# Two graph layers by Strassen products on one core: the next image's transposed h is turned and summed in another phase

## The chip, the cores and the metric

The kernel runs on one core of a Trainium2 chip. The metric is the device time in microseconds of one execution; three executions of the kernel before gave 2360.97, 2363.22 and 2365.91 us, and their median, 2363.22, is the time before. The profile is of one more execution, whose span was 2354.3 us.

## The reference

There are 32 independent images (the batch). Each has a 512 x 512 matrix `x` (nodes by features) and a 512 x 512 adjacency `adj`. Two layers follow each other; everything is in 32-bit floats.

```python
# x, adj: [32, 512, 512]; nodemask: [32, 512]; W: [512, 1024]; Wqk: [512, 1024]; Wv: [512, 512]
# layer 0
h   = maximum(layernorm(x), 0)                      # eps 1e-5, over features
deg = sum(adj, -1, keepdims=True)
agg = einsum('bij,bjf->bif', adj, h) / maximum(deg, 1e-6)
x1  = x + relu(einsum('bnf,of->bno', concatenate([h, agg], 2), W))
# layer 1
h1  = maximum(layernorm(x1), 0)
q, k = split(h1 @ Wqk, 2, -1)
v    = h1 @ Wv
agg  = einsum('bij,bjd->bid', adj, k * nodemask[:, :, None])
w    = nodemask / sqrt(512) * einsum('bid,bid->bi', q, agg)
out  = x1 + softmax(w, axis=1)[:, :, None] * v
```

## The kernel before

Each 512 x 512 product is one level of Strassen's scheme: seven products of 256 x 256 blocks instead of eight. The factors stand in "slots": four for the blocks and three more for sums of blocks. `left_sums` and `right_sums` make those sums with four adds or subtractions each.

```python
def left_sums(s, on=None):
    return [
        lambda: add(s(4), s(2), s(3), on), lambda: sub(s(6), s(0), s(2), on),
        lambda: sub(s(5), s(4), s(0), on), lambda: sub(s(2), s(1), s(5), on),
    ]

def product(name, terms, place, finish):
    def m(k, p, first):                 # product k: 4 matmuls for each term
        ...
        yield                           # a step ends here
    pp = mm_tile(f"pp_{name}")          # a PSUM tile [128, 2, 256]; the pool has 8
    yield from m(1, pp, True)
    c11 = place(0, 0)
    copy(c11, pp)                       # ScalarE
    pr = mm_tile(f"pr_{name}")
    yield from m(2, pr, True)
    finish(0, 0, c11, pr, c11)          # VectorE
    yield from m(6, pp, False)          # goes on in pp
    ...                                 # k = 5, 7, 3 in the same manner, with a third tile pq
    yield from m(4, pp, False)
    finish(1, 0, None, pp, None)        # VectorE's last read of pp

def run(phase, n, plan):
    for i in range(n):
        if phase is not None:
            next(phase)                 # the matmuls of step i
        for f in plan.get(i, []):       # what the plan hangs on step i, for all engines
            f()
```

For image i the main loop runs four phases. A phase is a stream of TensorE work in steps, and a `Plan` hangs other engines' instructions on the steps. Engines take their instructions in the order in which they are recorded.

- **O** (`layer0_out`, tiles `pp_o`, `pr_o`, `pq_o`; 14 steps): h·W1 and adj·Y, giving x1 in `xu`. Reads hT as the left factor.
- **V** (`layer1_tv`, tiles `ptv`; 14 steps): the "joint product" of image i-1, two levels of Strassen, h1 by Wqk's and Wv's product matrix, giving `tv`.
- **U** (`layer1_u`, 7 steps): adj·(masked h1) of image i, into the buffer that held x1.
- **Y** (`layer0_y`, 7 steps): h·W2 of image i+1. Reads hT and its sums.

`hT` is the transposed h of the next image, in one buffer (half of the constant tile `wide`). The rows of h are normalised, written to scratch in HBM, read back in another order (`to.read`), and then turned in 32 x 32 blocks on VectorE (`turn`, two halves); then four `sums` fill the slots of Strassen's sums. The adjacency (`aT`) and h1 (`h1T`) go the same way.

```python
class FrontH:                           # h of one image
    def turn(self, h):
        self.to.turn(h, hT)             # VectorE, L280 of the kernel
    def sums(self, i):
        left_sums(of(hT))[i]()          # VectorE, L94 and L97

class FrontH1:                          # x1 and h1 of one image
    def keep(self):                     # x1 to scratch, 1 MB: dx<-xu
        nc.sync.dma_start(out=self.x1, in_=X[self.b].rearrange("p c f -> p (c f)"))
    def write(self, c):                 # normalise a quarter (ScalarE), send it: dh1T<-h1m
        normalize(self.rows(c), ...)
        nc.sync.dma_start(out=self.to.d[c]..., in_=self.rows(c))
    def mask(self, c):                  # ScalarE, in place: waits for the store of the quarter
        nc.scalar.activation(self.rows(c), self.rows(c), AF.Copy, scale=mraw[:, c, self.b:self.b + 1])

def layer0_out(b, w1):
    def finish(r, c, o, p, s):
        dst = X[b][:, 2 * r:2 * r + 2, ts(c, H)]
        if s is not None:
            add(o, p, s)
            p = o
        nc.vector.scalar_tensor_tensor(dst, p, 0.0, dst, op0=ALU.max, op1=ALU.add)   # L442

def layer1_tv(b):                       # 7 products of 7 matmul pairs, in 4 PSUM tiles each
    ...
    yield from parts(1, pp, True, keep(0))     # keep: ScalarE copies out
    yield from parts(2, pr, True, plus(0))     # plus: VectorE adds from PSUM
    yield from parts(6, pp, False, keep(1))
    yield from parts(5, pq, True, keep5)
    yield from parts(7, pp, False, keep(3))
    for n in range(4):
        add(part(3, n), part(3, n), m5[n])
    yield from parts(3, pq, False, plus(1))
    yield from parts(4, pp, False, keep(2))
```

`Post` is what follows V for image i-1: `recombine` makes the blocks of `tv` from the products (seven adds for the query half of `tv`, and seven for its value half), `dot`, `scores` and the softmax, then `apply` scales the value rows, `add_x1` adds x1 by an accumulating DMA of GpSimd, and `store` writes the output.

Of the kernel before, what the change touches and what calls it, by code (L numbers as in the profile page):

```python
# [22 lines left out]
def kernel(  # L23
# [72 lines left out]
    def sub(o, a, b, on=None):  # L96
        (on or nc.vector).tensor_tensor(o, a, b, op=ALU.subtract)  # L97
# [11 lines left out]
    def right_sums(s, on=None):  # L109
        return [  # L110
            lambda: sub(s(4), s(1), s(0), on), lambda: sub(s(6), s(3), s(1), on),
            lambda: sub(s(5), s(3), s(4), on), lambda: sub(s(1), s(2), s(5), on),
        ]

    def of(t):
        return lambda i: t[:, i]
# [133 lines left out]
    def shift(t, a=0, b=C):  # L250
        mv, rstd, nmr = t
        nc.vector.scalar_tensor_tensor(  # L252
            nmr[:, a:b], mv[:, a:b, 0], -1.0, rstd[:, a:b], op0=ALU.mult, op1=ALU.mult
        )
# [391 lines left out]
    stream = Stream()  # L646
# [5 lines left out]
    def chain(p, f, n):  # L652


        p.at(n(0), f.stats, 2)
        p.at(n(0), shift, f.t, 0, 2)
        p.at(n(0), f.write, 0)
        p.at(n(1), f.stats, 3)
        p.at(n(1), variance, f.t, 2, 4)
        p.at(n(1), f.write, 1)  # L660
        p.at(n(2), shift, f.t, 2, 4)
        p.at(n(3), f.write, 2)
        p.at(n(3), f.mask, 0)
        p.at(n(4), f.write, 3)
        p.at(n(4), f.keep)
        p.at(n(4), f.mask, 1)
        p.at(n(5), f.masked_sums, 0)
        p.at(n(5), f.mask, 2)
        p.at(n(6), f.mask, 3)
# [179 lines left out]
    with tc.manual_schedule(engines=engines):  # L849
        weights, mvR = start()  # L850
        post = None
        for i in range(B):
            more, last = i + 1 < B, i + 1 == B
            if i > 0:

                p = Plan()
                right_y = right_sums(of(Y[i]), nc.gpsimd)
                p.at(0, right_y[0])
                p.at(0, right_y[2])
                for k in (1, 3):  # L860
                    p.at(1 + k // 2, FA[i].sums, k, nc.gpsimd)
                    p.at(1 + k // 2, right_y[k])
                if i == 1:
                    for k, g in enumerate(weights[4:]):
                        p.at(3 + 2 * k, g)
                    fa = FA[2]
                    for h in range(2):
                        for c in range(2):
                            p.at(2 * h + c, fa.sum, 2 * h + c)
                            p.at(4 + 2 * h + c, fa.write, 2 * h + c)  # L870
                        p.at(2 + 2 * h, fa.degrees, h)
                    FH[3] = FrontH(3)
                    p.at(9, FH[3].load, 0)
                    p.at(10, FH[3].load, 1)
                f1 = F1[i - 1]
                if post is not None:
                    for k in (5, 6):
                        p.at(0, post.recombine, k, None, 1)
                p.at(0, f1.turn, 0)
                p.at(1, f1.turn, 1)  # L880
                if post is not None:
                    for c in range(C):
                        p.at(2 + c, post.apply, c)
                    p.at(3, post.add_x1, 0)
                    p.at(5, post.add_x1, 1)
                    p.at(9, post.store, 0)
                    p.at(11, post.store, 1)
                for k in range(4):
                    p.at(2 + k, f1.sums, k)
                for k in range(4):  # L890
                    p.at(5 + k, f1.inner_sums, k, 0, 7)
                for n in range(4):
                    p.at(2 * n + 1, stream.load)
                if 1 < i and i + 2 < B:
                    fh = FH[i + 2]
                    for c in range(C):
                        p.at(7 + c, fh.stats, c)
                        p.at([11, 12, 13, 13][c], fh.write, c)
                    p.at(10, variance, fh.t)
                    p[11].insert(0, lambda t=fh.t: shift(t))  # L900
                if more:
                    th = FH[i + 1]
                    p.at(5, th.to.read, 0)
                    p.at(6, th.to.read, 1)
                    p.at(11, th.turn, 0)
                f = F1[i] = FrontH1(i)
                p.at(12, f.stats, 0)
                p.at(12, f.stats, 1)
                p.at(13, variance, f.t, 0, 2)
                run(layer0_out(i, stream.take), 14, p)  # L910


                post = Post(i - 1, F1[i - 1])
                p = Plan()
                p.at(0, f.stats, 2)
                p.at(0, shift, f.t, 0, 2)
                p.at(0, f.stats, 3)
                p.at(1, variance, f.t, 2, 4)
                if last:
                    p.at(1, FA[i].factor)  # L920
                p.at(3, shift, f.t, 2, 4)
                for c in range(C):
                    p.at([2, 3, 5, 6][c], f.write, c)
                    p.at([7, 7, 8, 9][c], f.mask, c)
                p.at(6, f.keep)
                for k in range(4):
                    p.at([9, 10, 10, 11][k], f.masked_sums, k)
                if i + 2 < B:
                    fa = FA[i + 2] = FrontA(i + 2)
                    p.at(2 if i > 1 else 11, fa.load, 0)  # L930
                    p.at(3 if i > 1 else 13, fa.load, 1)
                if i == 1:
                    fh = FH[3]
                    for c in range(C):
                        p.at(4 + c, fh.stats, c)
                        p.at(9 + c, fh.write, c)
                    p.at(7, variance, fh.t)
                    p[9].insert(0, lambda t=fh.t: shift(t))
                if more:
                    p.at(3, th.turn, 1)  # L940
                exchanged = FA[i + 1] if more else f
                p.at(6, exchanged.to.read, 0)
                p.at(7, exchanged.to.read, 1)
                for k in range(7):
                    p.at(12 + k // 4, post.recombine, k, 0, 0)
                run(layer1_tv(i - 1), 14, p)


            p = Plan()
            if i == 0:  # L950
                fh = FH[2]
                for c in range(C):
                    p.at(c, fh.stats, c)
                p.at(3, variance, fh.t)
                p.at(4, shift, fh.t)
                p.at(4, weights[0])
                p.at(5, fh.write, 0)
                p.at(6, fh.write, 1)
                p.at(5, weights[1])
                p.at(2, FA[1].to.read, 0)  # L960
                p.at(3, FA[1].to.read, 1)
            elif more:
                for k in range(7):
                    p.at(k // 4, post.recombine, k, 1, 0)
                for c in range(C):
                    p.at(2 + c // 2, post.dot, c)
                p.at(4, post.scores)
                p.at(4, post.maximum)
                for k in range(4):
                    p.at(5 + k // 2, th.sums, k)  # L970
                p.at(6, post.shift)
                if i + 2 < B:
                    late = 2 if i == 1 else 0
                    for c in range(C):
                        p.at(1 + c + late, fa.sum, c)
                    p.at(3 + late, fa.degrees, 0)
                    if i > 1:
                        p.at(5, fa.degrees, 1)
            else:
                p.at(0, f.turn, 0)  # L980
                for k in range(3):
                    p.at(1, f.inner_sums, k, 0, 2)
                p.at(1, f.turn, 1)
                for k in range(4):
                    p.at(2 + k // 2, f.sums, k)
                p.at(4, f.inner_sums, 3, 0, 2)
                for k in range(4):
                    p.at(5 + k // 2, f.inner_sums, k, 2, 7)
# [5 lines left out]
            if more:  # L994
                p = Plan()
# [5 lines left out]
                if i > 0:  # L1001
                    p.at(1, post.exponents)
                    p.at(2, post.row_sum)
                    p.at(4, post.weights)
                    for k in range(5):
                        p.at(3 + (k + 1) // 2, post.recombine, k, None, 1)
                p.at(2, FA[i].factor)
                if i == 0:
                    p.at(0, fh.write, 2)
# [22 lines left out]
        p = Plan()  # L1032
# [71 lines left out]
```

## Time and profile before

| | before |
|---|---|
| median of three | 2363.22 us |
| profiled span | 2354.3 us |
| TensorE clock granted, mean | 0.996 |
| TensorE, VectorE, ScalarE, GpSimd busy | 2263.0, 1946.8, 1078.4, 495.3 us |
| DMA moved | 463.65 MB, 197 GB/s over the span |
| `dx<-xu` (x1 to scratch), issue to landing | 6.3 us, 32 times |
| `dh1T<-h1m` (h1 to scratch), issue to landing | 3.2 us, 128 times |

In the profile an instruction is named by its engine, the line of the kernel, its operation and its tiles, `out<-in`, with buffer numbers left out. Where a helper records the instruction, the line is the helper's: L94 and L97 are all adds and subtractions, L100 all copies of ScalarE, L130 all matmuls but V's, L467 V's. `wide` holds hT, `shT` the rows of h that are to be turned into it, `xu` x and x1, `m_tv` the copies of V's product 5. A wait is put down to the instruction that released it last. TensorE's own time line is the one to read for the end of the program; a gap on another engine costs something only if TensorE waits for it later.

### The profile page before, as it was taken

The page shows a single profiled execution, that of the slowest core. Times are in us where ns is not written, and L with a number is a line of the kernel's source. Part 1 is how long each engine was busy: PE and PEld are TensorE (multiplying, and loading weights), DVE is VectorE, ACT ScalarE, POOL GpSimd, SP SyncE. Part 2 cuts the span into 40 slices and gives each one's busy share as a digit, 9 for nine tenths or more (in the row PEclk, how much of TensorE's full clock was granted, in tenths as well). Part 3 has the DMA queues.
Part 4 walks back from the last instruction along what each step waited for, and adds up shares of the span by engine and source line. Part 5 has one row for each costly group of instructions (what it writes and reads, how often), then busy time and mean ns, then how long its engine had stood idle before and what let it go on. Part 6 is the DMA issues. An engine that isn't in the chain of part 4 may idle for free.

```text
span 2354.3 us, 32391 instructions
## 1 busy us (share of the span) xinstructions
PE 2263.0 (96%) x10372; PEld 1966.8 (84%) x10372; DVE 1946.8 (83%) x3619; ACT 1078.4 (46%) x2031; POOL 495.3 (21%) x453
## 2 busy tenths in 40 slices
PE   7999999999999999999999999999999999999995
PEld 6788888888888888888888888888888888888884
DVE  6698788888898887898888988888888889888878
ACT  4454443544444544444444445444454444455332
POOL 0102222112222122222022221222220222211222
PEclk9999999999999999999999999999999999999998
DMA  9877877777978778777779787788777797877662
GB/s 219 229 198 182 229 199 197 202 199 187 240 185 200 205 184 216 215 191 202 194 184 242 184 202 202 182 217 213 195 200 199 182 240 189 202 198 199 144 161 67
DMA packets 409593, 463.65 MB, mean 197 GB/s; under 512 B 37680, under 2 KB 271152, under 8 KB 405328
## 3 DMA queue, kind: packets, MB, share of 16 engines
q1 hardware_dynamic: 400176, 428.56, 69.2%
q0 software_dynamic: 8928, 32.51, 7.4%
q8 instruction: 82, 1.34, 0.2%
q14 instruction: 87, 0.71, 0.1%
q10 hardware_dynamic: 320, 0.52, 0.1%
HBM read 293.93 MB, written 167.51 MB: 196 GB/s over the span
## 4 chain that ended last, share of the span: by engine, by line
DVE 37%; DMA 23%; PE 21%; ACT 10%; issue 3%; SPq 3%; POOL 2%; DVEq 0%; ACTq 0%; POOLq 0%
DVE tv L94 12%; DMA dh1T<-h1m 6%; PE pp_o L130 5%; PE pp_y L130 5%; DVE st L242 4%; ACT tv L100 4%; DMA tv<-dx 3%; DMA shT<-dhT 3%; DVE tv L541 3%; DMA sh1T<-dh1T 3%; PE ptv L467 3%; ACT h1m L258 3%; PE pq_y L130 3%; DMA daT<-a 3%; DVE h1T L97 3%
## 5 line engine op out<-in xcount | busy, mean ns | idle before, releaser
L467 PE MATMUL ptv<-mv,h1T 128*128 128x256 f32 x3136 | 690.5, 380 | 17.1 <-DVE xu L442 14.2
L467 PEld LDWEIGHTS ptv<-mv,h1T 128*128 128x128 f32 x3136 | 593.9, 190 | 108.5 <-DVE xu L442 26.0
L94 DVE TENSOR_TENSOR tv<-tv 128x256 f32<-128x256 f32 (+1 forms) x644 | 315.7, 518 | 10.6
L130 PE MATMUL pp_y<-wide 128*128 128x256 f32 x1024 | 245.8, 383 | 32.6 <-DVE wide L97 32.6
L100 ACT ACTIVATE tv<-ptv 128x512 f32<-128x512 f32 x496 | 241.3, 537 | 62.2 <-PE ptv L467 61.2
L97 DVE TENSOR_TENSOR h1T<-h1T 128x512 f32<-128x512 f32 (+2 forms) x195 | 259.6, 1344 | 1.2
L130 PEld LDWEIGHTS pp_y<-wide 128*128 128x128 f32 x1024 | 193.5, 191 | 68.0 <-issue 43.0
L130 PE MATMUL pp_o<-y,aT 128*128 128x256 f32 x1024 | 242.5, 380 | 1.0 <-POOL y L97 0.9
L130 PE MATMUL pp_u<-h1m,aT 128*128 128x256 f32 x1024 | 242.1, 379 | 1.4 <-ACT xu L100 1.4
L130 PE MATMUL pp_o<-w,wide 128*128 128x256 f32 x992 | 234.5, 379 | 2.3 <-DMA w<-dw 2.3
L130 PEld LDWEIGHTS pp_u<-h1m,aT 128*128 128x128 f32 x1024 | 194.7, 190 | 28.4 <-ACT xu L100 1.8
L130 PEld LDWEIGHTS pp_o<-y,aT 128*128 128x128 f32 x1024 | 194.2, 190 | 28.8 <-POOL y L97 2.9
L130 PEld LDWEIGHTS pp_o<-w,wide 128*128 128x128 f32 x992 | 188.7, 190 | 28.0 <-issue 2.7
L97 POOL TENSOR_TENSOR y<-y 128x512 f32<-128x512 f32 x124 | 194.8, 1571 | 18.4 <-DVE y L94 16.0
L550 POOL PARTITION_ALL_REDUCE gtop<-top x32 | 22.2, 692 | 824.7 <-DVE top L547 824.7
L100 ACT ACTIVATE o<-pp_o 128x512 f32<-128x512 f32 x96 | 57.3, 597 | 301.5 <-PE pp_o L130 301.5
L94 DVE TENSOR_TENSOR tv<-tv,m_tv 128x512 f32<-128x512 f32 x124 | 69.2, 620 | 141.9 <-ACT tv L100 138.9
L248 POOL TENSOR_TENSOR rstd<-rstd,mhalf 128x2 f32<-128x2 f32 (+1 forms) x96 | 78.4, 817 | 503.4 <-DVE rstd L247 503.4
L258 ACT ACTIVATE n<-n,nmr,rstd 128x512 f32<-128x512 f32 x120 | 88.3, 805 | 189.5 <-DVE nmr L252 134.5
L97 DVE TENSOR_TENSOR h1m<-h1m 128x512 f32<-128x512 f32 x128 | 85.3, 688 | 105.5 <-ACT h1m L379 105.5
L100 ACT ACTIVATE xu<-pp_u 128x512 f32<-128x512 f32 x128 | 76.4, 597 | 199.6 <-PE pp_u L130 195.9
L94 DVE TENSOR_TENSOR tv<-ptv,tv 128x512 f32<-128x512 f32 x248 | 142.2, 614 | 2.9 <-PE ptv L467 2.9
(113 smaller groups left out, 3458.7 us busy)
## 6 DMA issues: line engine op xcount, KB each, us to landing
w<-dw SPq DMA_DIRECT2D x217, 256.0 KB, 4.7
xu<-in_x_dram SPq DMA_DIRECT2D x128, 256.0 KB, 4.8
a<-in_adj_dram SPq DMA_DIRECT2D x256, 128.0 KB, 3.3
dh1T<-h1m SPq DMA_DIRECT2D x128, 256.0 KB, 3.2
dx<-xu SPq DMA_DIRECT2D x32, 1024.0 KB, 6.3
sh1T<-dh1T SPq DMA_DIRECT2D x256, 128.0 KB, 5.0
shT<-dhT SPq DMA_DIRECT2D x248, 128.0 KB, 4.2
daT<-a SPq DMA_DIRECT2D x124, 256.0 KB, 4.8
```

Of the source, the lines that this page charges most:

```text
L94: (on or nc.vector).tensor_tensor(o, a, b, op=ALU.add)
L97: (on or nc.vector).tensor_tensor(o, a, b, op=ALU.subtract)
L100: nc.scalar.activation(o, i, AF.Copy)
L130: nc.tensor.matmul(p[:, rc, :], lt[:, LEFT[k], dk, ts(rc, P)], right[:, dk, :], start=first and n == 0, stop=True, skip_group_check=True,)
L242: nc.vector.bn_stats(st, src)
L248: nc.gpsimd.tensor_tensor(rstd[:, a:b], rstd[:, a:b], mhalf[:, a:b], op=ALU.pow)
L258: nc.scalar.activation(o, i, AF.Relu, scale=t[1][:, c:c + 1], bias=t[2][:, c:c + 1])
L467: nc.tensor.matmul(banks[n][:, :, ts(i, P)], left[:, LEFT[k], LEFT_IN[j], :], mvR[:, RIGHT[k], RIGHT[j], :, :], start=first and i == 0, st ...
L541: nc.vector.scalar_tensor_tensor(v, v, 1.0, u, op0=ALU.mult, op1=ALU.mult, accum_out=self.acc[:, c:c + 1])
L550: nc.gpsimd.partition_all_reduce(self.gtop, self.top, channels=P, reduce_op=ReduceOp.max)
```

## The change

The diff moves pieces of work between phases, and adds or takes away none.

- The two turns of the next h go from O's step 11 and V's step 3 to V's steps 2 and 4.
- The four sums of the next h go from U's steps 5 and 6 to V's steps 6 and 7.
- The last two of seven adds for the value half of `tv` go from O's first step to Y, where the other five are; those start at the same step, one a half step closer.
- x1 is sent to scratch (`keep`) at V's step 1, before the four stores of h1, instead of at step 6 after them; for the first image, whose chain runs outside V, at its first step.
- The loads of the streamed weights in O keep their steps but come first within them.

Its aim is to have hT complete before Y needs it, and to relieve VectorE in O and U.

```diff
@@ chain (the first image)
+        p.at(n(0), f.keep)
         p.at(n(0), f.stats, 2)
...
         p.at(n(4), f.write, 3)
-        p.at(n(4), f.keep)
@@ O
                 p = Plan()
+                for n in range(4):
+                    p.at(2 * n + 1, stream.load)
...
-                if post is not None:
-                    for k in (5, 6):
-                        p.at(0, post.recombine, k, None, 1)
                 p.at(0, f1.turn, 0)
                 p.at(1, f1.turn, 1)
...
-                for n in range(4):
-                    p.at(2 * n + 1, stream.load)
...
                     p.at(5, th.to.read, 0)
                     p.at(6, th.to.read, 1)
-                    p.at(11, th.turn, 0)
@@ V
-                p.at(6, f.keep)
+                p.at(1, f.keep)
...
                 if more:
-                    p.at(3, th.turn, 1)
+                    p.at(2, th.turn, 0)
+                    p.at(4, th.turn, 1)
+                    for k in range(4):
+                        p.at(6 + k // 2, th.sums, k)
@@ U
-                for k in range(4):
-                    p.at(5 + k // 2, th.sums, k)
@@ Y
-                    for k in range(5):
-                        p.at(3 + (k + 1) // 2, post.recombine, k, None, 1)
+                    for k in range(7):
+                        p.at(3 + k // 2, post.recombine, k, None, 1)
```

## The prediction

> **What bounds the kernel now.** I read the busy shares first, then the waits of TensorE alone, then the timelines of TensorE and VectorE over one image in the middle of the run (Y at 1233.19, O at 1247.12, V at 1271.44 us).
>
> ```profile
> PE 2263.0 (96%) x10372; PEld 1966.8 (84%) x10372; DVE 1946.8 (83%) x3619; ACT 1078.4 (46%) x2031; POOL 495.3 (21%) x453
> ```
>
> TensorE is busy 96% of the span and nothing in the change takes a multiplication away, so the change can only fill the 4% in which it stands still. The waits of TensorE (engine, tile and line, what it waited for; us in total, times, longest):
>
> ```profile
> PE pp_y L130 <- DVE wide L97: 32.6, 28, 1.7
> PE ptv L467 <- DVE xu L442: 14.2, 26, 1.0
> ...
> PE pp_o L130 <- DMA w<-dw: 2.3, 1, 2.3
> ```
>
> The first is Y, once in each of 28 images: its third product wants hT's sums. The second is V, in 26 images: it wants a PSUM bank that O's last block still holds until VectorE has read it (L442). Both name VectorE. On TensorE's timeline (start, duration, instruction, idle before it):
>
> ```profile
> 1234.91 1.89 PE L130 MATMUL pr_y<-wide 128*128 128x256 f32 x8
> 1238.41 1.97 PE L130 MATMUL pp_y<-wide 128*128 128x256 f32 x8 [1.60 <-DVE wide L97]
> 1240.21 1.89 PE L130 MATMUL pq_y<-wide 128*128 128x256 f32 x8
> ...
> 1271.44 5.34 PE L467 MATMUL ptv<-mv,h1T 128*128 128x256 f32 x24
> 1277.37 16.24 PE L467 MATMUL ptv<-mv,h1T 128*128 128x256 f32 x74 [0.59 <-DVE xu L442]
> ```
>
> Undisturbed groups of 8 follow each other every 1.73 us. Here the step is 3.50, and the next 1.80: 1.84 lost for a wait shown as 1.60. In the next image a wait of 0.79 costs 1.02. So a wait costs itself and about 0.23 more. V's 98 matmuls want 98 x 1.727/8 = 21.15 us; this V took 22.01, the one before (1199.58 to 1221.10) 21.52. VectorE around the same places:
>
> ```profile
> 1199.89 1.25 DVE L280 STREAM_TRANSPOSE wide<-shT 128x1024 f32<-128x1024 f32 x1
> ...
> 1204.29 0.69 DVE L442 SCALAR_TENSOR_TENSOR xu<-pp_o,xu 128x512 f32<-128x512 f32 x1
> ...
> 1213.16 0.69 DVE L97 TENSOR_TENSOR h1m<-h1m 128x512 f32<-128x512 f32 x1 [2.85 <-ACT h1m L379]
> 1219.45 2.23 DVE L94 TENSOR_TENSOR tv<-tv,m_tv 128x512 f32<-128x512 f32 x4 [5.59 <-ACT tv L100]
> ...
> 1235.51 0.68 DVE L94 TENSOR_TENSOR wide<-wide 128x512 f32<-128x512 f32 x1
> 1236.11 0.69 DVE L97 TENSOR_TENSOR wide<-wide 128x512 f32<-128x512 f32 x1
> ...
> 1237.58 1.41 DVE L97 TENSOR_TENSOR wide<-wide 128x512 f32<-128x512 f32 x2
> ```
>
> VectorE runs nearly without a gap from 1219 us through U, Y and O to the early part of the next V, and then stands still for 2.85 and 5.59 us inside V. The turn at 1199.89 stands ahead of the read that V's bank waits for (1204.29), and the four sums end at 1238.9 because they stand behind V's adds and the dots. So V has spare VectorE time, and O and U have none.
>
> **The Trainium skill.** "Perfetto Trace Analysis", Optimization Strategy, says to look for the gaps on the most contended engine, find which instruction releases it, and make that start sooner; it adds that interleaving regimes with different bounds can help. The trace agrees: TensorE's gaps name two VectorE instructions. "VectorE: DVE Perf Modes", on the TRN2 errata, gives (N+151)/0.96 ns for an fp32 add, 691 ns at N=512; the rows above show 0.68 and 0.69 us, 0.61 to the next start. "PSUM — Partial Sum Buffer", Specifications, gives 8 banks of 2 KiB; a 128x512 fp32 tile is one bank. O leaves one tile unread and V takes eight at once; the wait stands before the matmul of V's eighth tile, after 24 matmuls, so the trace agrees. "DMA: Bandwidth & Descriptors", Queues, rings and completion order, says that each engine consumes one queue's descriptors in ring order. That matters for x1, below.
>
> **The change part by part.** No work is added or removed; all of it moves.
>
> (1) The four sums leave U: 4 x 0.61 = about 2.5 us, with a transpose start-up some 2.7, and go into V's steps 6 and 7. By TensorE's rate those lie 9 to 11 us after V's start, before the 2.85 and 5.59 us gaps, and these two hold 8.4 us. Y then has hT before V ends. Gain: the whole of Y's wait, 32.6 + 28 x 0.23 = 39 us. I keep 37.
>
> (2) The first turn leaves O step 11 for V step 2, the second goes from V step 3 to V step 4. L442's read of pp_o comes 1.25 us sooner, at about V+4.2 instead of V+5.4 (1204.98 less 1199.58), where the eighth tile is due at V + 24 x 0.216 = V+5.2. The second turn now stands behind V's last two adds of its second product, not ahead of them. V loses 14.2 + 26 x 0.25 = 20.7 us today, between 0.2 and 1.2 in one image, so 1.25 us covers it. I keep 14: with the wait gone TensorE comes to V's last product sooner, and that has no margin. It needs the banks that ScalarE copies at 1216.98 to 1219.4, and TensorE asks for them from V + 84 x 0.216 = V+18.1, 1217.7, onwards.
>
> (3) Two of seven adds of `tv` (2 x 0.61 us) go from O's start to Y. In Y VectorE has the 2.7 us of the sums back, so it ends Y's own adds no later against TensorE. O's h1T turns wait for a DMA today (1.42 us at 1252.38); that wait grows to some 2.7 us, since VectorE comes earlier, but it ends at the same place against O's start. Nothing on the path.
>
> (4) x1's store is issued before the four h1 stores instead of after them. The DMA share in the two us after VectorE's last write to x1:
>
> ```profile
> 1205.00:1207.00 2.00, 1.98 (x9) 1.77 (x10) 1.89 (x7) 1.01 (x2) 0.16 (x1) 1.00 0.00 0
> ```
>
> The last two fields are the DMA share and GB/s: the DMA engines stand still for 2 us just there. x1 is 1 MB; between its issue at 1213.42 and its landing lie 6.3 us by the page, and at the 270 to 370 GB/s of busy stretches it is 3 to 4 us of transfer. Half of it or more fits the hole. The rest stands ahead of the h1 stores, on which ScalarE's masking waits:
>
> ```profile
> 1216.35 0.72 ACT L379 ACTIVATE h1m<-h1m,mraw 128x512 f32<-128x512 f32 x1 [2.47 <-DMA dh1T<-h1m]
> ```
>
> Against that, part 2 lets the first h1 rows be normalised 1.25 us sooner (their shift waits behind L442's read on VectorE), so the issues that follow move up as well. I take the two as equal: 1.75 MB of h1 stores and adjacency loads stand behind x1 until that mask, about 6 us at 290 GB/s, from 1209.5 to 1215.6 where today it is 1216.3. Gain 0, with an error of 1 us an image either way.
>
> (5) Weight loads are issued first within O's odd steps. The wait of 2.3 us for `w<-dw`, once, may go; so may three short waits of O for GpSimd's sums of y (0.9 us by the same table). I keep 2.
>
> Sum: 37 + 14 + 2 = 53 us of a ceiling of 39 + 20.7 + 3.2 = 63. From 2363 that gives 2310, and 2311 is my number.
>
> **The rivals.** *ScalarE takes the place of VectorE in V.* The mask at 1216.35 waits for a store, the copies of V's product stand behind it in ScalarE's order, and TensorE's last product in V needs their banks at once. If x1 delays the store by 1 us, V loses up to 1 us in 28 images: 28 us back, and a time near 2338. For it: part 2's missing margin, and the mask's wait of 2.47 us. Against: the DMA hole, and no wait of TensorE for ScalarE in V in the present table.
>
> *VectorE is the bound, and the wait only moves.* From 1219.45 to the read of pp_o in the next V (its start is 1271.44 + 5.9) lie 57.9 us of VectorE's order with under 3 us of gaps. Taking away 2.7 and 1.25 leaves 54; TensorE's undisturbed image is 12.09 (Y, 7 groups of 1.727) + 24.17 (O, 14) + 21.15 (V) + 12.09 (U) = 69.5 us, which leaves 69.5 + 5.2 - 19.9 = 54.8. So it fits by under 1 us: if V's adds start 1 us later, half of V's wait comes back (10 us, 2320). The busy windows say the same: 60.2 us of VectorE's work between 1175 and 1247, 72 us, become 60.2 in 69.5, 87%.
>
> *Early issue disturbs more than it helps.* The x1 store may hold back not only masks but the adjacency rows and the reads at V's steps 6 and 7. Those reads are needed in Y, 20 us on, so I give this little.
>
> *GpSimd.* Its sums of y begin some 8.5 us after its all-reduce of the exponents' sums, which starts at 1243.40:
>
> ```profile
> 1251.87 0.19 POOL L339 TENSOR_TENSOR wd<-deg,mcol 128x4 f32<-128x4 f32 x1 [7.72 <-ACT o L100]
> ```
>
> If O moved up against it, O would wait for y. But the all-reduce waits for VectorE's `es`, which stands behind the sums and comes 2.7 us sooner where O comes 1.84 sooner. So this should not bind.
>
> **Range and chances.** Y's part is nearly certain, since sums placed in a gap 20 us ahead cannot be late; alone it makes 2326. V's part and the x1 store carry the doubt. All found: 2301. V's gain eaten by ScalarE or DMA: 2325 to 2338. I give 2311, 2300 to 2338 for 8 in 10. The 2% line is 2316: faster by over 2% 0.58, within 2% 0.38, slower 0.04.
>
> **What would show it.** Right: no wait of Y for `wide` in TensorE's table; Y 12.09 us from start to start in all middle images; VectorE's turns and sums of `wide` within V, and its gaps there smaller by 5 us; `xu<-pp_o` read by V+4.3; h1 stores landing within 1 us of where they do now against V. Wrong: a new line in which `ptv` waits for ScalarE's `tv` or `m_tv`; a wait of `pp_u` for the `h1m` sums; longer idle time of ScalarE's mask before `dh1T`; or O's h1T sums running into V. A time above 2340 would mean that x1's store delays the masks by over 1 us.

## The result and the profile after

The changed kernel takes 2417.47 us (median of 4, 2411.24 to 2419.49) against 2362.91 us before: ratio 1.0225, 95% interval 1.0204 to 1.0247. It is slower, where 2311 us was predicted. The profiled span grew from 2354.3 to 2417.5 us.

The busy shares of the changed kernel, and its waits of TensorE (engine, tile and line, what it waited for; us in total, times, longest):

```profile
PE 2285.4 (95%) x10372; PEld 1987.6 (82%) x10372; DVE 1925.0 (80%) x3619; ACT 1085.2 (45%) x2031; POOL 472.9 (20%) x453
```
```profile
PE pp_o L130 <- DMA w<-dw: 70.2, 24, 4.7
PE pp_o L130 <- ACT n L258: 18.5, 6, 3.5
...
PE ptv L467 <- DVE xu L442: 0.4, 1, 0.4
```

Both waits that the change aimed at are gone: no line names `wide`, and V's for L442's read is down to one of 0.4 us. In their place stands one that was not there before. O waits for a streamed weight, 24 times by name, and 6 times more put down to `n`; ScalarE had long been done with that, and the weight landed last there too. Added up from start to start on TensorE's timeline, the phases of all images took, in us (V without that of the last image):

| | before | after | difference |
|---|---|---|---|
| Y | 427.8 | 387.7 | -40.1 |
| V | 677.8 | 657.5 | -20.3 |
| O | 778.6 | 901.1 | +122.5 |
| U | 388.4 | 389.6 | +1.2 |

One O of the changed kernel on TensorE's timeline (start, duration, instruction, idle before it); it starts at 1199.84:

```profile
1218.83 1.89 PE L130 MATMUL pq_o<-y,aT 128*128 128x256 f32 x8
1223.34 1.97 PE L130 MATMUL pp_o<-w,wide 128*128 128x256 f32 x8 [2.61 <-DMA w<-dw]
1226.86 21.32 PE L467 MATMUL ptv<-mv,h1T 128*128 128x256 f32 x98
```

It is O's seventh product, hence the last of the seven weight tiles. The product is due 12 groups of 1.727 = 20.7 us after O's start. V behind it runs its full length without a gap. GpSimd and the queue of SyncE in the same O:

```profile
1193.66 0.75 POOL L560 PARTITION_ALL_REDUCE gs<-es  x1 [5.85 <-DVE es L559]
...
1202.18 0.19 POOL L339 TENSOR_TENSOR wd<-deg,mcol 128x4 f32<-128x4 f32 x1 [7.77 <-DVE h1T L285]
...
1211.16 1.97 POOL L575 DMA_DIRECT2D tv<-dx  x2
```
```profile
1209.08 3.85 SPq L212 DMA_DIRECT2D shT<-dhT  x8
1213.02 0.47 SPq L409 DMA_DIRECT2D w<-dw  x1
```

L575 is `add_x1`: two transfers of 0.5 MB that add x1 to the output in SBUF. GpSimd issues them as soon as its sums of y are done. Before, that was here, in the O that starts at 1247.12:

```profile
1261.30 1.96 POOL L575 DMA_DIRECT2D tv<-dx  x2
```

So the transfer moved from 14.2 to 11.3 us after O's start, with the whole chain of GpSimd: its all-reduce starts 6.2 us ahead of O where it was 3.7. Now it overlaps the 1 MB of reads of the next h's rows (issued from 9.2 to 13.1 us) and the last weight load behind them. The issues in 7 us of that place, with KB and median us to landing, before (1255 to 1262) and after (1208 to 1215):

```profile
shT<-dhT SPq DMA_DIRECT2D x8, 128.0 KB, 4.2
w<-dw SPq DMA_DIRECT2D x2, 256.0 KB, 4.0
tv<-dx POOLq DMA_DIRECT2D x1, 512.0 KB, 5.9
```
```profile
shT<-dhT SPq DMA_DIRECT2D x8, 128.0 KB, 4.4
tv<-dx POOLq DMA_DIRECT2D x2, 512.0 KB, 9.4
w<-dw SPq DMA_DIRECT2D x2, 256.0 KB, 6.5
```

Over 29 images the last weight landed, on average, 18.2 us after O's start before and 23.8 after.

### The profile page after: what moved, and what is told of

It reads as the page before. It is cut to its first block, busy times and chain, and to the rows that moved or that the text cites. A ratio compares the mean times of both kernels' runs of the same rounds, so it can differ in the third digit from the quotient of the medians.

```text
span 2417.5 us, 32420 instructions
## 1 busy us (share of the span) xinstructions
PE 2285.4 (95%) x10372; PEld 1987.6 (82%) x10372; DVE 1925.0 (80%) x3619; ACT 1085.2 (45%) x2031; POOL 472.9 (20%) x453
## 4 chain that ended last, share of the span: by engine, by line
PE 71%; DMA 17%; DVE 6%; SPq 3%; issue 1%; ACT 1%; POOL 1%; DVEq 0%; POOLq 0%; ACTq 0%
PE ptv L467 25%; PE pp_o L130 12%; DMA w<-dw 10%; PE pp_u L130 9%; PE pp_y L130 8%; PE pq_u L130 4%; PE pq_y L130 3%; PE pr_o L130 3%; SPq L212 2%; PE pr_u L130 2%; PE pr_y L130 2%; PE pq_o L130 2%; DVE tv L94 1%; DMA tv<-dx 1%; DMA sh1T<-dh1T 1%
## 5 line engine op out<-in xcount | busy, mean ns | idle before, releaser
L467 PE MATMUL ptv<-mv,h1T 128*128 128x256 f32 x3136 | 683.1, 379 | 3.1 <-DVE h1T L97 2.7
L100 ACT ACTIVATE tv<-ptv 128x512 f32<-128x512 f32 x496 | 252.8, 546 | 313.0 <-PE ptv L467 312.3
L130 PE MATMUL pp_o<-w,wide 128*128 128x256 f32 x992 | 258.0, 407 | 88.8 <-DMA w<-dw 70.2
L94 DVE TENSOR_TENSOR tv<-tv 128x256 f32<-128x256 f32 (+1 forms) x644 | 321.1, 518 | 12.7
L130 PEld LDWEIGHTS pp_o<-w,wide 128*128 128x128 f32 x992 | 198.0, 202 | 128.4 <-ACT n L258 70.0
L130 PE MATMUL pp_o<-y,aT 128*128 128x256 f32 x1024 | 252.2, 391 | 0.0
L97 DVE TENSOR_TENSOR h1T<-h1T 128x512 f32<-128x512 f32 (+2 forms) x195 | 235.4, 1221 | 1.2
L130 PEld LDWEIGHTS pp_o<-y,aT 128*128 128x128 f32 x1024 | 204.4, 200 | 31.3
L97 POOL TENSOR_TENSOR y<-y 128x512 f32<-128x512 f32 x124 | 182.7, 1473 | 16.5 <-DVE y L94 14.1
L100 ACT ACTIVATE y<-pp_y 128x512 f32<-128x512 f32 x128 | 76.5, 597 | 189.6 <-PE pp_y L130 189.6
L94 DVE TENSOR_TENSOR tv<-ptv,tv 128x512 f32<-128x512 f32 x248 | 147.8, 620 | 12.6 <-PE ptv L467 12.6
```

Of the source, the lines that this page charges most:

```text
L94: (on or nc.vector).tensor_tensor(o, a, b, op=ALU.add)
L100: nc.scalar.activation(o, i, AF.Copy)
L130: nc.tensor.matmul(p[:, rc, :], lt[:, LEFT[k], dk, ts(rc, P)], right[:, dk, :], start=first and n == 0, stop=True, skip_group_check=True,)
L467: nc.tensor.matmul(banks[n][:, :, ts(i, P)], left[:, LEFT[k], LEFT_IN[j], :], mvR[:, RIGHT[k], RIGHT[j], :, :], start=first and i == 0, st ...
```

## The experiments

All ratios are to the kernel before, run on the same chip; the bracket is the 95% interval. "Issue of x1" and "weight" are the averages over 29 images of the issue of `add_x1` and of the landing of the last weight, in us from O's start; the weight is needed at 20.7.

| run | us | ratio | issue of x1 | weight |
|---|---|---|---|---|
| kernel before | 2362.9 | 1 | 14.8 | 18.2 |
| changed kernel | 2417.5 | 1.0225 [1.0204, 1.0247] | 11.1 | 23.8 |
| a1 late scaling | 2342.7 | 0.9911 [0.9896, 0.9926] | 17.4 | 19.3 |
| a2 before, x1 added early | 2429.7 | 1.0282 [1.0264, 1.0299] | 10.6 | 23.8 |
| a3 x1 stored late | 2409.6 | 1.0193 [1.0173, 1.0213] | 11.2 | 23.6 |
| a4 sums back in U | 2348.8 | 0.9941 [0.9926, 0.9955] | 14.7 | 18.2 |
| b1 reads after weight | 2337.7 | 0.9901 [0.9886, 0.9916] | 12.8 | 17.3 |
| b2 b1 and x1 stored late | 2299.1 | 0.9740 [0.9724, 0.9755] | 11.3 | 18.0 |
| b3 plain copy | 2358.6 | 0.9999 [0.9983, 1.0015] | 11.3 | 22.4 |
| b4 scaling in the middle | 2345.0 | 0.9930 [0.9913, 0.9946] | 12.7 | 21.3 |
| c1 a1 and x1 stored late | 2294.0 | 0.9717 [0.9698, 0.9736] | 16.1 | 18.3 |
| c2 before, x1 stored early | 2375.2 | 1.0063 [1.0046, 1.0079] | 14.3 | 18.6 |
| c3 before, reads after weight | 2360.4 | 1.0001 [0.9991, 1.0010] | 14.7 | 15.2 |
| d1 turns, sums, late scaling | 2294.6 | 0.9717 [0.9701, 0.9733] | 16.2 | 18.3 |

**a1, late scaling.** `add_x1` waits for ScalarE's scaling of the rows, so scaling later delays it.

```diff
-                        p.at(2 + c, post.apply, c)
-                    p.at(3, post.add_x1, 0)
-                    p.at(5, post.add_x1, 1)
+                        p.at(8 + c // 2, post.apply, c)
+                    p.at(8, post.add_x1, 0)
+                    p.at(9, post.add_x1, 1)
```

> The changed kernel, with the scaling of the value rows moved from O's steps 2 to 5 to its steps 8 and 9, and with it the accumulating transfer of x1 that waits for it (issued about 16 us after O's start instead of 11.1). Theory (the transfer of x1 collides with the last weight load of O): the weight load lands about 18 us after O's start again, the waits of O for it vanish, Y and V stay at 12.09 and 21.15 us, time about 2300 us (2294 to 2310). Rival (x1's early store to scratch, or the order of the weight loads, slows the DMA): the wait stays, about 2417 us.

75 us came back, and the waits for the last weight with them, save one of 1.7 us. But 2300 was expected. What is left are waits of O's fourth product for its weight (tile `pq_o`; 27.6 us, 25 times) and of V for ScalarE's `tv` (6.4 us, 11 times), of which the changed kernel has 0.2 us and none: a second fault, open at this point.

**a2, before with x1 added early.** The kernel before, where GpSimd issues `add_x1` ahead of its last two sums, nothing else on TensorE, VectorE or the queue reordered; the scaling moves up by one step.

```diff
+                    late_by = 3 if k == 3 and post is not None else 0
-                    p.at(1 + k // 2, FA[i].sums, k, nc.gpsimd)
-                    p.at(1 + k // 2, right_y[k])
+                    p.at(1 + k // 2 + late_by, FA[i].sums, k, nc.gpsimd)
+                    p.at(1 + k // 2 + late_by, right_y[k])
...
-                        p.at(2 + c, post.apply, c)
-                    p.at(3, post.add_x1, 0)
-                    p.at(5, post.add_x1, 1)
+                        p.at(1 + c, post.apply, c)
+                    p.at(2, post.add_x1, 0)
+                    p.at(4, post.add_x1, 1)
```

> The kernel before, with only GpSimd's order changed: the two accumulating transfers of x1 are issued ahead of its last two sums, about 11 us after O's start instead of 14.7. Theory: O waits for the last weight load as in the changed kernel, 3 to 4 us an image in 29 images, time 2450 to 2490 us (the waits of Y and V stay). Rival: no wait for weights, about 2363 us.

TensorE's waits in this run:

```profile
PE pp_o L130 <- DMA w<-dw: 91.8, 30, 3.9
...
PE pp_y L130 <- DVE wide L97: 2.9, 3, 1.1
```

The loss appears without any of the moved work. This makes the early transfer sufficient. The time is 20 us under what was expected, and the second line says why: Y's wait fell from 32.6 to 2.9 us and V's vanished, with the sums still in U. That VectorE gets ahead while TensorE stands in O fits this and was not tried by itself.

**a3, x1 stored late** (the `keep` line of V back from step 1 to step 6).

> The changed kernel with x1's store to scratch back at V's step 6, after the h1 stores. Theory: nothing of the loss goes, waits of O for the weight load as in the changed kernel, 2405 to 2425 us. Rival (the early store is the cause): the waits vanish, about 2300 us.

The wait stays (66.8 us and 16.2 by the two names). x1's store is not its cause.

**a4, sums back in U** (the two added lines of sums in V removed, the two of U restored).

> The changed kernel with the four sums of the next h back in U's steps 5 and 6, the turns left in V. Theory: the sums delay the exponents' sums on VectorE, hence GpSimd's chain and the accumulating transfer, by about 2.7 us, to about 13.5 us after O's start; most of O's wait goes and Y's wait of 39 us comes back, 2335 to 2365 us. If the sums have nothing to do with O's wait: 2417 + 39 = about 2456 us.

The transfer is back at 14.7, the weight lands in time, and Y waits again, 43.4 us in 29 images. So it is the sums' move out of U that lets GpSimd's chain come forward. V keeps its gain (657.7 us in all): that belongs to the turns.

**b1, reads after the weight load, and b2, the same with x1 stored late.**

```diff
-                    p.at(5, th.to.read, 0)
-                    p.at(6, th.to.read, 1)
+                    p.at(7, th.to.read, 0)
+                    p.at(8, th.to.read, 1)
```

> The changed kernel with one order swapped on the queue: the reads of the next h's rows are issued after O's last weight load instead of ahead of it. The accumulating transfer of x1 still starts at about 11 us after O's start. Theory (the last weight load is late because it stands behind 1 MB of reads that the accumulating transfer slows): the load is issued about 12.2 us after O's start, as soon as its buffer is free, and lands by 18.5, ahead of 20.7 where it is needed; O has no wait, time 2294 to 2315 us. If the transfer slows the load whatever stands ahead of it: it lands after 21, time over 2350 us.

> The same with x1's store to scratch back at V's step 6. If x1's early store is neutral: within 5 us of the run before it. If it delays the h1 stores and ScalarE's masks, as the late-scaling run's 6.4 us of V waiting for ScalarE suggest: 5 to 15 us faster.

The last weight lands in time in both, although the transfer still starts at 12.8 and 11.3. Yet b1 missed its range, and b2 shows the second fault: x1's early store costs 38.5 us, where 5 to 15 were expected. In b1, TensorE waits

```profile
PE pq_o L130 <- DMA w<-dw: 18.5, 20, 2.3
...
PE ptv L467 <- ACT tv L100: 12.6, 16, 1.4
```

of which b2 has 1.2 us and nothing. ScalarE's waits of its masks for the h1 stores, in b1 and in b2:

```profile
ACT h1m L379 <- DMA dh1T<-h1m: 97.3, 66, 2.9
```
```profile
ACT h1m L379 <- DMA dh1T<-h1m: 36.4, 34, 2.2
```

The third h1 store, for which the third mask waits, lands 17.1 us after V's start in b1 and 14.8 in b2 (averages of 25 images). That ScalarE's copies stand behind this mask and TensorE needs their banks is the chain of the prediction's first rival. The other wait is of O's fourth product, due 6 groups or 10.4 us after O's start: its weight is issued at 6.5 us and lands at 10.5 in b1, against 5.2 and 9.2 in b2 (averages of 31 images). What makes the queue later against O was not tried.

**b3, plain copy.** `accum_op` taken out of `add_x1`: x1 overwrites the value rows, so the output of all images but the last leaves out the second layer's term.

> The changed kernel with x1 copied over the value rows by the same GpSimd transfers without accumulation, so that the output lacks the second layer's term for all images but the last. Same bytes read, same time of issue. If the bytes beside the reads are the cause: O's wait stays, 2400 us or more. If the accumulating form is (it takes about 11 us for 1 MB in the changed kernel): the transfer lands within 6 us, the weight load lands before 21 us after O's start, time under 2350 us.

Between the two: O waits 51 us for weights instead of 89, and the weight lands at 22.4. By these waits a plain transfer of the same size, issued at the same time, does more than half of the harm, and the accumulating form adds the rest. In the profiles of b3 and of the changed kernel 0.5 MB takes 7.6 us from issue to landing as a plain copy (median) and 8.6 accumulating.

**b4, scaling in the middle** (as a1, at steps 6 and 7).

> The changed kernel with the scaling of the value rows at O's steps 6 and 7, so that the transfer of x1 is issued about 12.5 and 13.7 us after O's start, between the changed kernel (11.1) and the late scaling (17). Theory: by then most of the reads are issued, and the weight load lands at 19 to 21.5; O's waits mostly vanish, and the start of the next stages is not put off as with the late scaling: 2305 to 2350 us. If any accumulating transfer in flight beside the weight load costs the same: 2400 us or more.

The time and the landing are in their ranges, but O's waits did not mostly vanish: 33 us in 26 waits are left, and that in the profile of the fastest run (2333.2 us). With a2, the changed kernel and a4 it gives a series: transfer issued at 10.6, 11.1, 12.7, 14.7, weight landed at 23.8, 23.8, 21.3, 18.2. a1 stands outside it (17.4 and 19.3), with the second fault in it.

**c1, late scaling and x1 stored late.** The edits of a1 and a3 together.

> The changed kernel with the late scaling (accumulating transfer at about 16 us) and with x1's store back at V's step 6. Theory (two separate faults: the early transfer in O, and the early x1 store that shows only once O is free of its wait): both gone, no wait of V for ScalarE's tv and few of O for weights, 2295 to 2312 us. If the late scaling itself puts off what follows: about 2340 us as with the late scaling alone.

The busy line and TensorE's waits of c1 (the first is in the prologue):

```profile
PE 2249.7 (98%) x10372; PEld 1970.1 (86%) x10372; DVE 1904.6 (83%) x3619; ACT 1082.1 (47%) x2031; POOL 469.2 (20%) x453
```
```profile
PE h L637 <- ACT h L709: 14.1, 2, 13.6
...
PE pp_o L130 <- DMA w<-dw: 0.8, 1, 0.8
```

This is 2.8% faster than before, 5.1% faster than the changed kernel, and by the ratios some 46 us faster than a1, which differs by x1's early store alone: a second measurement of that fault. V takes 21.15 us in every image but the first, and Y 12.09.

**c2, before with x1 stored early.**

> The kernel before with x1's store alone moved to V's step 1. Theory: the h1 stores behind it land later, ScalarE's masks and its copies of V follow, and part of it reaches TensorE as V's waits for tv, less than the 38 us found without the other waits, since V and Y have waits of their own here: 2368 to 2400 us. If the early store is neutral by itself: 2358 to 2367 us.

The size was right and the path was not. V waited for `tv` 0.9 us in all; four O's waited for the weight (7.4 us), and Y's wait rose from 32.6 to 40.1. Six of this run's waits, of 1.97 to 2.56 us, also set off the half clock described at the end. How the store brings the waits about is open.

**c3, before with the reads after the weight load.**

> The kernel before with the reads of the next h's rows issued after O's last weight load. Theory: the weight load had no wait to lose here (it lands at 18.1, needed at 20.7), so nothing is won: 2356 to 2368 us; the reads land by about 24 us, at the time of the first turn in O, so some of VectorE's work may be late, up to 2385. If the swap by itself were what makes the fastest version fast: about 2300 us.

No change. Of the two places where it was tried, the swap is worth something only where the transfer is early.

**d1, only turns, sums and late scaling**, on the kernel before.

> The kernel before with only the turns and the sums of the next h moved into V, and the scaling of the value rows at O's steps 8 and 9 so that the transfer of x1 keeps its place. The adds for the value half stay in O, the weight loads keep their order, x1's store stays late. Theory (the other parts of the change bring nothing): the same as the fastest version so far, 2288 to 2302 us, no waits of Y for wide or of V for L442's read. If the adds in O's first step or the order of the weight loads matter: 5 us or more slower than that, with waits of V for the read of pp_o.

As fast as c1 (2293.6 to 2296.6 against 2293.7 to 2294.1). The adds for the value half and the order of the weight loads bring nothing that shows in the total. The latter has its place once: the second image's O waits 2.4 us for a weight here and 0.8 us in c1.

## Why the prediction was wrong

**Part 1, right.** Y gained 40.1 us against a ceiling of 39 and 37 kept. VectorE's timeline of the changed kernel around V (from 1226.86) shows the moved work in place:

```profile
1229.78 1.25 DVE L280 STREAM_TRANSPOSE wide<-shT 128x1024 f32<-128x1024 f32 x1
...
1233.79 1.23 DVE L280 STREAM_TRANSPOSE wide<-shT 128x1024 f32<-128x1024 f32 x1
1235.05 0.69 DVE L94 TENSOR_TENSOR wide<-wide 128x512 f32<-128x512 f32 x1
1235.66 2.01 DVE L97 TENSOR_TENSOR wide<-wide 128x512 f32<-128x512 f32 x3
1239.82 0.69 DVE L97 TENSOR_TENSOR h1m<-h1m 128x512 f32<-128x512 f32 x1 [2.14 <-ACT h1m L379]
1243.54 2.23 DVE L94 TENSOR_TENSOR tv<-tv,m_tv 128x512 f32<-128x512 f32 x4 [3.03 <-DMA saT<-daT]
```

Both gaps inside V are still there after the sums, shorter by 3 us together where 5 was foretold.

**Part 2, right, and more than kept.** V gained 20.3 us of a ceiling of 20.7, where 14 was kept. In c1, where no stall in O lends time, V still runs at 21.15: with x1 stored late, ScalarE's copies are in time. There the profiled span is 62.2 us shorter than before (66.8 by the medians of that chip), against the prediction's ceiling of 63: what the moved work gives back was judged rightly.

**The step that failed: the rival "GpSimd".** It said that `es`, for which the all-reduce waits, "comes 2.7 us sooner where O comes 1.84 sooner. So this should not bind." It followed that chain to the sums of y, which TensorE reads and which indeed did not bind, and stopped there. The chain ends in the issue of `add_x1`, 1 MB of DMA on which nothing urgent waits. Its earlier start hurts a transfer on another queue, and the sum of the parts had no term for it: O was to gain 2 us and lost 122.5. The term is made of 88.7 us of waits in 30 images, 30 x 0.23 = 7 of restart, and some 30 us of half clock (below), less some 5 that O had lost before. The margin was readable: the weight landed at 18.2 and was due at 20.7, 2.5 us to spare, right behind reads of which the last was issued 1 us ahead of the transfer. The net shift of the all-reduce was too small as well: 2.5 us against O in the images shown, not 0.9. The sign "A time above 2340 would mean that x1's store delays the masks" named the wrong cause for this loss. Without it the time would still have been above the stated range of 2300 to 2338, at 2342.7 (a1), because of part 4.

"DMA: Bandwidth & Descriptors" of the Trainium skill, Issuing engines are not separate DMA queues, says that transfers issued by SyncE, ScalarE or GpSimd run on the same 16 engines and interleave. The runs agree: GpSimd's transfer moved a landing on SyncE's queue by 5.6 us. I had cited the page's ring order for x1's store alone.

**Part 4, wrong in size, and hidden.** "I take the two as equal. Gain 0" put x1's store and the earlier start of h1 at par. They are not: the third h1 store lands 2.3 us later (b1 against b2), and the early store costs 38.5 us there and some 46 in a1 against c1, where O has no wait for its last weight, save one in a1. In the changed kernel itself it showed as only 8 us, with runs that overlap (a3): while O stands, VectorE finishes x1 earlier against V (1.1 us after its start, 3.4 in b1), the store leaves 1.1 us after V's start instead of 4.9 as in b1, and the third h1 store lands at 13.5 us with it and at 13.4 without (averages of 31 images). The rival that had this mechanism (ScalarE in V's place) allowed 28.

**Parts 3 and 5** were put on no path or at 2 us; d1 agrees within its noise.

## What to carry over

When an engine is relieved, follow its chain to everything it issues, transfers without an urgent reader too, and look what lands with little margin at the new place. A wait that disappears may have kept two transfers apart, and a new wait may hide a second fault: a2 and a3 show other waits shrink while TensorE stands. So remove the largest wait first, then judge the remaining parts of a change again, each by itself.

## What the runs showed of the hardware

A wait of TensorE of 2 to 4 us can cost some 1.7 us more than itself. The granted clock (third field from the end) after one of 3.19 us in the changed kernel, and TensorE's timeline there:

```profile
2260.00:2262.00 2.00, 0.00 (x0) 0.00 (x0) 1.90 (x5) 0.00 (x0) 0.00 (x0) 1.00 1.04 350
2262.00:2264.00 2.00, 1.88 (x6) 1.58 (x7) 0.29 (x2) 0.00 (x0) 0.74 (x1) 0.66 0.77 233
2264.00:2266.00 2.00, 2.00 (x6) 1.54 (x5) 0.00 (x0) 0.00 (x0) 0.00 (x0) 0.50 0.00 1
2266.00:2268.00 2.00, 2.00 (x11) 1.75 (x10) 0.47 (x1) 0.00 (x0) 0.00 (x0) 0.99 0.00 0
```
```profile
2262.12 3.25 PE L130 MATMUL pp_o<-w,wide 128*128 128x256 f32 x8 [3.19 <-DMA w<-dw]
2265.16 2.33 PE L130 MATMUL pp_o<-y,aT 128*128 128x256 f32 x8
```

The clock is halved for about 3.4 us, and the two groups up to V's start at 2267.33 take 5.21 us instead of 3.45. By the matmuls' starts, a gap loses these 1.7 us or nothing. 18 gaps of the changed kernel do, hence the 30 us.

The length of a gap does not settle which. Over all fourteen traces, behind the prologue, no gap under 1.93 us loses them and all 20 above 3.42 us do; between, one of 2.40 us in the changed kernel did and one of 3.21 did not. The place settles it. By the clock records of the changed kernel, the halved stretches last 3.413 us each (the first, twice that) and start whole multiples of 3.413 us apart: those at 931.43, 1149.89 and 1296.66 lie 64 and 43 such windows from one another. Cutting the eleven traces that have such a stretch before the end into these windows sorts the gaps of 0.3 us and more: all 69 that left 0.585 of one window idle, or more, lost the 1.7 us; none of the 257 that left under 0.56 did; 6 of the 10 between did. So about 2 us of standing still within one window was enough.

"TensorE: Matmul & The Clock Gate" of the Trainium skill, What's actually happening, states a half clock after an idle window of about 3.4 us, a return after a busy window of that length, and windows that run freely. The length and the free-running windows agree with these traces; that the whole window must be idle does not, and there the traces decide.
